# A convolution and bidirectional-scan kernel: order of the first loads, taps scaled in one operation, and additions moved to VectorE in the lone fronts

## The chip, the cores and the metric

The kernel runs on one core of a Trainium2 chip. The metric is the device time of one launch in microseconds (us); lower is better. The engines are named as in the profile: PE is TensorE (matmuls), PEld its weight loads, DVE is VectorE, ACT is ScalarE, POOL is GpSimd, SP is SyncE, which computes nothing here and issues every DMA. A queue named with a trailing q (SPq, POOLq) is an engine's sequencer.

## The reference, cut to what matters

The input is a batch of 8 images of 64 channels and 128 x 128 pixels, fp32. Two layers follow each other. Layer 0 is a filter whose nine weights per pixel come from the image itself:

```python
h = conv(x, w1, b1, pad=1); h = where(h >= 0, h, 0.2 * h)
w_lp = softmax(conv(h, w2, b2), axis=1)          # 9 weights per pixel
w_hp = delta - w_lp                               # delta: 1 at the center tap
high = sum over 9 taps of shifted(x) * w_hp[tap]
x = x + high
```

Layer 1 normalizes over the channels, runs two bidirectional Mamba blocks over the 16384 pixels as a sequence, and ends with a residual convolution, a depthwise gate and a feed-forward part (FFN):

```python
x_norm = ln4d(input); seq = layernorm(tokens(x_norm))
for i in range(2): seq = bimamba_block(seq, ...)  # projections, conv1d of 4 taps, selective scan both ways
x = input + dw2(dw1(x_norm)) * (resconv(rmsnorm(seq)) + res)
x = x + ffn_out(gelu(g1) * g2)                    # g1, g2 = halves of depthwise3x3(ffn_in(ln4d(x)))
```

## The kernel before, in words

The whole program is one function, `tile_conv_seq_kernel`. It has three parts, one after the other.

**Constants.** Identity matrices, selection matrices and small vectors are made on VectorE and GpSimd. Each image buffer in DRAM has a border of zeros; `clear(x_img)` (L98, the DMA at L89) writes the zeros of the input's buffer with one DMA of 4257.5 KB, and it is the second DMA that SP issues. Then 24 small bias and norm vectors are loaded (L165 to L168).

**Weight preparation** (L188 to L358). The weights come in their natural layout and must be transposed, paired and scaled. Helpers do this: `twice` writes a weight twice side by side (one half by VectorE, L198, one by ScalarE, L199); `turned` (L204) is a matmul against the identity, or against a diagonal, which transposes and scales at once; `diagonal` (L215) builds on VectorE an identity scaled by a column of taps. For the nine FFN taps and the four taps of the scan's short convolution each tap takes one `diagonal`, one `turned` and one copy out of PSUM. The prepared weights of the front, of the mixing stage and of the FFN are stored to DRAM (`w_dram`, L289) for later loading; those of the scan stay on the chip. The scan's weights are prepared in two layers with two directions each, so in four units, with a head for each layer. In this part the order of the instructions is left to the scheduler. Its tiles lie in pools that are closed at the end of the part, and whose memory is used again.

**The stages.** Everything after that is planned in a dictionary: `at(time, phase, fn)` puts a step under a time and a phase, and the steps are issued in sorted order within `tc.manual_schedule()`, which keeps exactly this order on each engine. Scan chunks begin at time 0 and take the rest of the span. Around them lie four kinds of work: `Front` (layer 0 and the first normalization, L480 to L677), the scan (`Chunk`), `Mix` and `Ffn`. An image has NCH = 16 front chunks, planned FRONT_STEP = 24 apart. The front of image 0 begins at time -199, so its first eight chunks run before any scan chunk; these have `alone` set and hold two of their PSUM tiles in the pool `pw`, of which the scan has no use yet.

A front chunk works on 4 + 4 rows of the image. Its steps, in the names of the profile: `copy_x` (L681; 16 DMAs for an image, which copy the input into the bordered buffer), loads of two shifted windows (xa, L414), `hp` (L422 and L427, the first convolution, six groups of matmuls), `ha`/`hv` on ScalarE, `lp` (L510, L511, the logits), a softmax on VectorE, ScalarE and GpSimd (L517 to L538), `tp` (L543, transposes), `wt` on ScalarE (L547). Then for each of nine taps: `weight` spreads the tap's weights over the channels by a matmul (`wb`, L557), `weighted` multiplies them with the shifted window xb on VectorE (`t`, L561), and `gather` adds the product into PSUM by a matmul with the identity (`acc`, L566). `filtered` copies the sum out on ScalarE (`x1`, L570). Then follow the normalizations: center (`cp`, L577), means (`ms`, L452), root (`r`, on GpSimd, L461), spread (`rb`, L467) and scaling (`hc`, L585), with the pointwise convolution `dwp` (L594) between. Steps of neighbouring chunks interleave: the taps of one chunk stand beside the `hp` and `lp` of the next and the later norms of the one before.

The zeros of the border of another image buffer (`dw`, 15 DMAs at L89) are planned among the loads of the first chunks; each has 292.5 KB, the last 162.5 KB.

SP issues DMAs in program order. Each DMA signals one of eight semaphores in turn, and a DMA waits for the one that used its semaphore before, so at most eight are under way. A DMA whose destination reuses a tile waits on SP for the last user of this tile, and all DMAs behind it on SP wait too.

Of the kernel before, what the change touches and what calls it, by code (L numbers as in the profile page):

```python
# [8 lines left out]
F32 = mybir.dt.float32  # L9
# [6 lines left out]
P = 128  # L16
C = 64
# [38 lines left out]
def kernel(ctx: ExitStack, tc: tile.TileContext, a: dict, out: bass.AP):  # L56
# [38 lines left out]
    dw_img = [image(f"dw{i}") for i in range(2)]  # L95
    zero = const([C, PW], "zero")
    nc.vector.memset(zero, 0.0)
    clear(x_img)  # L98
# [89 lines left out]
    with tc.tile_pool(name="wspill", bufs=1) as fp, tc.tile_pool(name="wprep", bufs=2) as pp, \  # L188
            tc.tile_pool(name="wps", bufs=4, space=PSUM) as pps:
        wt = [fp.tile([P, n], F32, tag=f"w{i}", name=f"w{i}") for i, n in enumerate((FRONT_W, MIX_W, FFN_W))]  # L190
        w1_pair, w1_last, dw1 = front_weights(wt[0])
        (dw2_pair, dw2_last), (wres_pair, wres_last) = mix_weights(wt[1])
        wpair, wlast, wout_a, wout_b, win_b, wtap_b = ffn_weights(wt[2])

        def twice(src, n, m, k=1):

            t = pp.tile([n, k, 2, m], F32, tag=f"twice{k * m}", name="twice")
            nc.vector.tensor_copy(t[:, :, 0, :], src.rearrange("n (m k) -> n k m", k=k))  # L198
            nc.scalar.copy(t[:, :, 1, :], src.rearrange("n (m k) -> n k m", k=k))  # L199
            return t.rearrange("n k h m -> n k (h m)")  # L200

        def turned(lhsT, rhs, m, n):
            t = pps.tile([P, N], F32, tag="wps", name="turned")
            nc.tensor.matmul(t[0:m, 0:n], lhsT, rhs, start=True, stop=True)  # L204
            return t

        def to_blocks(dst, t, k, n):

            half = dst.shape[1] // 2
            nc.vector.tensor_copy(dst[0:k, 0:n], t[0:k, 0:n])  # L210
            nc.scalar.copy(dst[k : 2 * k, half : half + n], t[k : 2 * k, 0:n])

        def diagonal(col, n):
            d = pp.tile([P, P], F32, tag="diag", name="diag")
            nc.vector.tensor_scalar(d[0:n, 0:n], ident[0:n, 0:n], col, None, ALU.mult)  # L215
            return d[0:n, 0:n]

        both = pp.tile([P, C], F32, tag="both", name="both", bufs=1)
        nc.vector.tensor_tensor(both, ident[:, 0:C], ident[:, C:P], ALU.add)
        for t in wt:  # L220
            nc.gpsimd.memset(t, 0.0)
        nc.gpsimd.memset(w2a, 0.0)
        nc.gpsimd.memset(w2v[0:64, :], 0.0)

        w1n = pp.tile([32, C * 9], F32, tag="w1n", name="w1n")
        nc.sync.dma_start(w1n, a["L0_conv_w1"].rearrange("o c i j -> o (c i j)"))
        w1t = twice(w1n, 32, C, 9)
        resn = pp.tile([C, C * 9], F32, tag="resn", name="resn")
        nc.sync.dma_start(resn, a["L1_conv_resconv_w"].rearrange("o c i j -> o (c i j)"))
        resv = twice(resn, C, C, 9)  # L230
        dw2n = pp.tile([P, 9], F32, tag="dw2n", name="dw2n")
        for h in range(2):
            nc.sync.dma_start(
                dw2n[h * C : (h + 1) * C, :], a["L1_conv_dw2_w"].rearrange("c o i j -> c (o i j)")
            )
        for k in range(9):
            i, j = divmod(k, 3)
            t1 = turned(w1t[:, k, :], ident[0:32, 0:32], P, 32)
            tr = turned(resv[:, k, :], ident[0:C, 0:C], P, C)
            if j < 2:  # L240
                lo = slice(C * j, C * j + C)
                nc.vector.tensor_copy(w1_pair[lo, i, :], t1[lo, 0:32])
                nc.scalar.copy(wres_pair[lo, i, :], tr[lo, 0:C])
                nc.vector.tensor_scalar(dw2_pair[lo, i, :], ident[lo, lo], dw2n[lo, k : k + 1], None, ALU.mult)
            else:
                nc.vector.tensor_copy(w1_last[:, i, :], t1[:, 0:32])
                nc.scalar.copy(wres_last[:, i, :], tr[:, 0:C])
                nc.vector.tensor_scalar(dw2_last[:, i, :], both, dw2n[:, k : k + 1], None, ALU.mult)
        w2n = pp.tile([9, 32], F32, tag="w2n", name="w2n")
        nc.sync.dma_start(w2n, a["L0_conv_w2"].rearrange("o c i j -> o (c i j)"))  # L250
        to_blocks(w2a, turned(twice(w2n, 9, 32)[:, 0, :], ident[0:9, 0:9], 64, 9), 32, 9)
        nc.vector.tensor_scalar(w2v[0:64, :], w2a, 0.6, None, ALU.mult)
        nc.vector.tensor_scalar(w2a, w2a, 0.4, None, ALU.mult)
        dw1n = pp.tile([C, C], F32, tag="dw1n", name="dw1n")
        nc.sync.dma_start(dw1n, a["L1_conv_dw1_w"].rearrange("o c i j -> o (c i j)"))
        to_blocks(dw1, turned(twice(dw1n, C, C)[:, 0, :], ident[0:C, 0:C], P, C), C, C)

        fw = a["L1_conv_ffn_in_w"].rearrange("o c i j -> o (c i j)")  # L260
        fd = a["L1_conv_ffn_dw_w"].rearrange("o c i j -> o (c i j)")
        outn = pp.tile([C, HID], F32, tag="outn", name="outn")
        nc.sync.dma_start(outn, a["L1_conv_ffn_out_w"].rearrange("o c i j -> o (c i j)"))
        nc.scalar.copy(wout_a, turned(outn[:, 0:P], ident[0:C, 0:C], P, C)[:, 0:C])
        t = turned(outn[:, P:HID], ident[0:C, 0:C], REST_HID, C)
        for h in range(2):
            nc.scalar.copy(wout_b[C * h : C * h + REST_HID, :], t[0:REST_HID, 0:C])
        for g, c0, r0, n in ((0, 0, 0, P), (1, 0, HID, P), (2, 0, HID + P, REST_HID), (2, C, P, REST_HID)):
            fn = pp.tile([P, C], F32, tag="fn", name="fn")
            nc.sync.dma_start(fn[0:n, :], fw[r0 : r0 + n, :])  # L270
            fdn = pp.tile([P, 9], F32, tag="fdn", name="fdn")
            nc.sync.dma_start(fdn[0:n, :], fd[r0 : r0 + n, :])
            if g == 2:

                nc.scalar.copy(win_b[:, c0 : c0 + n], turned(fn[0:n, :], ident[0:n, 0:n], C, n)[0:C, 0:n])
                for h in range(2):
                    k0 = 9 * (c0 > 0)
                    nc.sync.dma_start(wtap_b[C * h : C * h + n, k0 : k0 + 9], fd[r0 : r0 + n, :])
            fn2 = twice(fn[0:n, :], n, C)[:, 0, :]
            for k in range(9):  # L280
                i, j = divmod(k, 3)
                t = turned(fn2, diagonal(fdn[0:n, k : k + 1], n), P, n)
                if j < 2:
                    lo = C * j
                    nc.vector.tensor_copy(wpair[lo : lo + C, i, g, c0 : c0 + n], t[lo : lo + C, 0:n])
                else:
                    nc.vector.tensor_copy(wlast[:, i, g, c0 : c0 + n], t[:, 0:n])
        for src, dst in zip(wt, w_dram):
            nc.sync.dma_start(dst, src)  # L289


        sel_d = fp.tile([P, G, P], F32, tag="sel_d", name="sel_d")
        negmask = fp.tile([P, G], F32, tag="negmask", name="negmask")
        nc.vector.tensor_reduce(
            negmask.rearrange("p (n o) -> p n o", o=1), ident.rearrange("p (d n) -> p n d", n=G), AX.X, ALU.add
        )
        nc.vector.tensor_scalar(negmask, negmask, -1.0, None, ALU.mult)
        for g in range(G):
            nc.vector.tensor_copy(
                sel_d[:, g, :].rearrange("k (d n) -> k d n", n=G),  # L300
                ident[:, 32 * g : 32 * g + 32].rearrange("k (d o) -> k d o", o=1).to_broadcast([P, 32, G]),
            )

        for l in range(DEPTH):
            nw = pp.tile([P, 1], F32, tag="nw", name="nw")
            for h in range(2):
                nc.sync.dma_start(nw[h * C : (h + 1) * C, :], row(a["L1_conv_m_norm_w"][l]))
            inx = pp.tile([DI, C], F32, tag="inx", name="inx")
            nc.sync.dma_start(inx, a["L1_conv_in_proj_w"][l, 0:DI, :])
            inz = pp.tile([DI, C], F32, tag="inz", name="inz")  # L310
            nc.sync.dma_start(inz, a["L1_conv_in_proj_w"][l, DI : 2 * DI, :])
            inx2 = twice(inx, DI, C)[:, 0, :]
            t = turned(twice(inz, DI, C)[:, 0, :], ident, P, DI)
            nc.vector.tensor_scalar(wz[:, l, :], t[:, 0:DI], nw, None, ALU.mult)
            on = pp.tile([C, DI], F32, tag="on", name="on")
            nc.sync.dma_start(on, a["L1_conv_outproj_w"][l])
            for g in range(2):
                to_blocks(
                    wo[:, l, g].rearrange("p i c -> p (i c)"),
# [160 lines left out]
    class Front:  # L480
# [82 lines left out]
        def gather(self, k):  # L563
            if k == 0:
                self.acc = acc_tile("acc")
# [772 lines left out]
```

## Time and profile before

| what | value |
|---|---|
| time, median of 3 runs | 29515.6 us (29510.37 to 29532.13) |
| the profiled execution's own time | 29464.12 us |
| its span | 29462.3 us |
| mean clock granted to PE | 0.866 of full |
| busy: POOL, DVE, PE, ACT | 94%, 93%, 80%, 63% |
| first weight load issued (w1n, L226) | 39.96 us |
| first instruction of weight preparation, last one | 41.79 us, 123.3 us |
| copies of image 0 issued | 111.09 to 140.8 us |
| first hp, first tap product | 155.52 us, 184.69 us |
| x1 copied out (L570), lone chunks | 201.31, 247.58, 292.23, 336.80, 381.28, 428.39, 472.98, 524.76 us |
| first operation of the scan on POOL, on DVE | 529.84 us, 539.04 us |

The profiled execution is one run; its time stands 51 us below the median of the three timed runs. A table of stretches gives for each the busy time of every engine with the number of its instructions, the clock, and the share of time in which the DMA engines were busy. A timeline row gives the start, the duration, the engine, the line, and what is written from what; in square brackets stands how long the engine was idle before it, and what ended this. A row of the waits gives the waiting instruction, what it waited for, the sum in us, the number of times and the longest.

### The profile page before, as it was taken

How to read it: one execution, taken by the hardware profiler on the slowest of the kernel's cores; microseconds unless marked ns; L12 is line 12 of the kernel's file. 1: busy time of each engine (PE TensorE's matmuls, PEld its weight loads, DVE VectorE, ACT ScalarE, POOL GpSimd, SP SyncE). 2: the span in 40 equal slices, each digit the busy share in tenths (PEclk: the TensorE clock that was granted, in tenths of full speed). 3: DMA queues.
4: the chain of work that ended last, by engine and by line, in shares of the span. 5: the costliest groups of instructions: out<-in, count | busy, mean ns of one | idle time of the engine just before them, and what ended most of it. 6: DMA issues, size and time to landing. Idle time of an engine off the chain costs nothing. (4 is left out here: it accounts for less than half of the span.)

```text
span 29462.3 us, 312607 instructions
## 1 busy us (share of the span) xinstructions
PE 23428.5 (80%) x97852; PEld 7363.8 (25%) x97852; DVE 27280.7 (93%) x17559; ACT 18566.1 (63%) x28357; POOL 27653.4 (94%) x8732
## 2 busy tenths in 40 slices
PE   7666888878788787887878878787787878878678
PEld 3211222223222232222322223222222222222123
DVE  4999999999999999999999999999999999999997
ACT  3666666666666666666666666666666666666663
POOL 3999999999999999999999999999999999999993
PEclk8777888988889888988889888898888988889789
DMA  4676677767777677776787767777677776777674
GB/s 114 221 245 219 226 246 242 240 217 230 249 241 237 216 234 254 239 233 217 235 256 235 233 219 237 251 239 229 221 239 247 236 228 219 246 246 238 217 250 142
DMA packets 2592281, 6762.83 MB, mean 230 GB/s; under 512 B 431270, under 2 KB 736822, under 8 KB 2589462
## 3 DMA queue, kind: packets, MB, share of 16 engines
q1 hardware_dynamic: 2590614, 6742.83, 70.7%
q8 instruction: 774, 12.68, 0.2%
q14 instruction: 893, 7.32, 0.1%
HBM read 5509.49 MB, written 1265.19 MB: 230 GB/s over the span
## 5 line engine op out<-in xcount | busy, mean ns | idle before, releaser
L1089 POOL TENSOR_TENSOR bu<-dup,bp 128x2048 f32<-128x2048 f32 x4096 | 18584.8, 4543 | 373.6 <-DVE w L1117 231.0
L1097 ACT ACTIVATE w<-dtp,a_neg 128x1024 f32<-128x1024 f32 x8192 | 9159.6, 1118 | 793.8 <-DVE hs L1115 334.7
L1136 POOL TENSOR_TENSOR hs<-hs,cp 128x1024 f32<-128x1024 f32 x2832 | 6693.9, 2364 | 236.0 <-ACT state L1129 183.1
L1139 DVE TENSOR_TENSOR hs<-w,cp 128x1024 f32<-128x1024 f32 x5360 | 6562.4, 1224 | 317.2 <-DMA cp<-bc_dram 88.5
L1117 DVE TENSOR_TENSOR_SCAN w<-w,state,bu 128x1024 f32<-128x1024 f32 x2683 | 6290.5, 2345 | 302.1 <-ACT w L1097 301.0
L1115 DVE TENSOR_TENSOR_SCAN w<-w,state,bu 128x1024 f32<-128x1024 f32 x2677 | 6278.7, 2345 | 250.2 <-ACT w L1097 248.8
L1155 PE MATMUL y<-hs,sel_y 128*32 128x512 f32 x32768 | 5126.6, 701 | 55.3 <-POOL hs L1136 55.1
L1129 ACT COPY state<-w 128x1 f32<-128x1 f32 x5360 | 838.0, 156 | 5484.9 <-DVE hs L1139 5433.5
L1117 DVE TENSOR_TENSOR_SCAN hs<-w,state,bu 128x1024 f32<-128x1024 f32 x1413 | 3308.4, 2341 | 183.3 <-issue 121.2
L1115 DVE TENSOR_TENSOR_SCAN hs<-w,state,bu 128x1024 f32<-128x1024 f32 x1419 | 3321.2, 2340 | 38.6 <-PE y L1155 17.5
L1148 PE MATMUL y<-xc,dskip 128*64 128x512 f32 x4096 | 1571.0, 856 | 1656.3 <-ACT yv L1172 1383.9
L967 PE MATMUL xp<-hn,wx 128*128 128x512 f32 x4096 | 2353.8, 704 | 653.6 <-ACT xc L973 476.2
L799 PE MATMUL fp<-fw,bgw 128*128 128x512 f32 (+1 forms) x5760 | 2272.1, 636 | 105.9 <-ACT ga L846 66.2
L1129 ACT COPY state<-hs 128x1 f32<-128x1 f32 x2832 | 541.2, 191 | 1937.8 <-DVE hs L1117 989.9
L1155 PEld LDWEIGHTS y<-hs,sel_y 128*32 128x32 f32 x32768 | 730.1, 117 | 3666.8 <-issue 2458.0
L1008 PE MATMUL dp<-xc,wdt 128*128 128x512 f32 x2048 | 1226.9, 683 | 463.8 <-ACT dt L1015 373.0
L461 POOL TENSOR_TENSOR r<-r,neg_half 128x8 f32<-128x8 f32 x768 | 1265.8, 1649 | 318.2 <-ACT r L458 299.2
L1097 ACT ACT_TABLE_LOAD x1134 | 1454.9, 1283 | 20.5
L566 PE MATMUL acc<-t,ident 128*128 128x512 f32 x2304 | 1370.9, 680 | 99.3 <-DVE hc L585 94.7
L805 PE MATMUL fp<-fw,bgw 64*128 64x512 f32 (+1 forms) x5760 | 1415.1, 609 | 0.0
L1045 POOL TENSOR_TENSOR dt<-dt,xc 128x1024 f32<-128x1024 f32 x512 | 1214.9, 2373 | 173.2 <-DMA dt_dram<-dt 154.7
L967 PEld LDWEIGHTS xp<-hn,wx 128*128 128x128 f32 x4096 | 830.6, 216 | 1967.7 <-issue 961.4
(211 smaller groups left out, 25729.1 us busy)
## 6 DMA issues: line engine op xcount, KB each, us to landing
bp<-bc_dram SPq DMA_DIRECT2D x4096, 256.0 KB
dup<-du_dram SPq DMA_DIRECT2D x4096, 256.0 KB
dtp<-dt_dram SPq DMA_DIRECT2D x4096, 256.0 KB
cp<-bc_dram SPq DMA_DIRECT2D x4096, 256.0 KB
hn<-hn_dram SPq DMA_DIRECT2D x1024, 256.5 KB
dt_dram<-dt SPq DMA_DIRECT2D x512, 512.0 KB
du_dram<-dt SPq DMA_DIRECT2D x512, 512.0 KB
yf_dram<-yv SPq DMA_DIRECT2D x512, 256.0 KB
```

Of the source, the lines that this page charges most:

```text
L799: nc.tensor.matmul(o, wpair[:, i, g, m], self.win[h][:, i : i + ROWS, 0:W], start=(i == 0), stop=False)
L805: nc.tensor.matmul(o, wlast[rows, i, g, m], self.win[h][rows, i : i + ROWS, lo : W + lo], start=False, stop=(i == 2),)
L967: nc.tensor.matmul(self.xp[h], wx[:, self.l, self.d, i, :], self.hn2[:, s.start + 2 * i : s.stop + 2 * i], start=(i == 0), stop=(i == 1),)
L1089: nc.gpsimd.tensor_tensor(bu, self.dup[self.pairs[k][1]], self.over_pair("bp", k), ALU.mult)
L1097: nc.scalar.activation(w, self.dtp[gp][:, i, :], AF.Exp, scale=a_neg[:, self.l, self.d, g, j : j + 1])
L1115: nc.vector.tensor_tensor_scan(to, w, bu, s0, ALU.mult, ALU.add)
L1117: nc.vector.tensor_tensor_scan(to[:, ::-1], w[:, ::-1], bu[:, ::-1], s0, ALU.mult, ALU.add)
L1129: nc.scalar.copy(self.column(u), h[:, T - 1 : T] if self.d == 0 else h[:, 0:1])
L1136: nc.gpsimd.tensor_tensor(hs, hs, c, ALU.mult)
L1139: nc.vector.tensor_tensor(hs, w, c, ALU.mult)
L1148: nc.tensor.matmul(self.y[C * h : C * h + C, :], dskip[:, self.l, self.d, C * gp : C * gp + C], self.xc[:, s], start=True, stop=False,)
L1155: nc.tensor.matmul(self.y[lo : lo + 32, :], sel_y, hs[:, i, s], start=False, stop=(k % 4 == 3))
```

## The change

It has three parts.

1. *Order of the loads.* `clear(x_img)` is taken from the constants. The weight preparation is put within `tc.manual_schedule()`, so its instructions keep the order in which they are written. At its beginning stand all loads of the front, mixing and FFN weights; behind them on SP the clear and the 16 copies of image 0; then the rest: the tap loads of the FFN (`wtap_b`), the stores of the prepared weights, the loads of the scan's weights. `plan_front` copies the image only for the later images. The tiles `fn` and `fdn` have four buffers instead of two.
2. *Taps.* `diagonal` is gone. `by_taps` multiplies a block of rows with all its taps in one VectorE operation (128 x 1152 for the FFN, 128 x 512 for the scan's convolution), and `turned` then transposes each tap's part against the identity. The copies of the third column of FFN taps (`wlast`) go from VectorE to ScalarE.
3. *Additions.* In a lone front chunk `gather` no longer uses TensorE: the first product's tile becomes `x1`, and each further product is added to it on VectorE. There is no copy out of PSUM for these chunks. In the other chunks nothing changes.

```diff
@@ constants
+    def copy_x(b, i):
+        r = W // NCH
+        nc.sync.dma_start(pixels(x_img)[:, 1 + r * i : 1 + r * i + r, 1 : W + 1], x[b, :, r * i : r * i + r, :])
     nc.vector.memset(zero, 0.0)
-    clear(x_img)
@@ weight preparation, now within tc.manual_schedule()
-        def diagonal(col, n):
-            d = pp.tile([P, P], F32, tag="diag", name="diag")
-            nc.vector.tensor_scalar(d[0:n, 0:n], ident[0:n, 0:n], col, None, ALU.mult)
-            return d[0:n, 0:n]
+            def by_taps(rows, taps, n, k):
+                m = rows.shape[1]
+                t = pp.tile([P, k, m], F32, tag=f"taps{k}", name="taps")
+                nc.vector.tensor_tensor(
+                    t[0:n], rows.rearrange("n (o m) -> n o m", o=1).to_broadcast([n, k, m]),
+                    taps.rearrange("n (k o) -> n k o", o=1).to_broadcast([n, k, m]), ALU.mult,
+                )
+                return t[0:n]
...
+            for part in ((0, 0, 0, P), (1, 0, HID, P), (2, 0, HID + P, REST_HID), (2, C, P, REST_HID)):
+                _, _, r0, n = part
+                fn = pp.tile([P, C], F32, tag="fn", name="fn", bufs=4)
+                nc.sync.dma_start(fn[0:n, :], fw[r0 : r0 + n, :])
+                fdn = pp.tile([P, 9], F32, tag="fdn", name="fdn", bufs=4)
+                nc.sync.dma_start(fdn[0:n, :], fd[r0 : r0 + n, :])
+                parts.append((part, fn, fdn))
+            clear(x_img)
+            for i in range(NCH):
+                copy_x(0, i)
...
-            fn2 = twice(fn[0:n, :], n, C)[:, 0, :]
+                fn2 = by_taps(twice(fn[0:n, :], n, C)[:, 0, :], fdn[0:n, :], n, 9)
-                t = turned(fn2, diagonal(fdn[0:n, k : k + 1], n), P, n)
+                    t = turned(fn2[:, k, :], ident[0:n, 0:n], P, n)
-                    nc.vector.tensor_copy(wlast[:, i, g, c0 : c0 + n], t[:, 0:n])
+                        nc.scalar.copy(wlast[:, i, g, c0 : c0 + n], t[:, 0:n])
...
-                    t = turned(inx2, diagonal(cw[:, j : j + 1], DI), P, DI)
+                    taps = by_taps(inx2, cw, DI, KC)
+                        t = turned(taps[:, j, :], ident, P, DI)
@@ class Front
         def gather(self, k):
+            if self.alone and k == 0:
+                self.x1 = self.t.pop(k)
+            elif self.alone:
+                nc.vector.tensor_tensor(self.x1, self.x1, self.t.pop(k), ALU.add)
+            if self.alone:
+                return
             if k == 0:
                 self.acc = acc_tile("acc")
             nc.tensor.matmul(self.acc, ident, self.t.pop(k), start=(k == 0), stop=(k == 8))
         def filtered(self):
-            self.x1 = tmp("x1")
-            nc.scalar.copy(self.x1, self.acc)
+            if not self.alone:
+                self.x1 = tmp("x1")
+                nc.scalar.copy(self.x1, self.acc)
@@ plan_front
-        for i in range(NCH):
+        for i in range(NCH if b else 0):
             at(a - FRONT_STEP - 24 + i, REST, copy_x, b, i)
```

## The prediction

> **What bounds the kernel now.** I read first the table of busy time by stretches of the span (length, busy time of PE, PE loads, DVE, ACT and POOL, then clock, DMA share, GB/s).
>
> ```profile
> 0.00:42.00 42.00, 0.00 (x0) 0.00 (x0) 8.24 (x32) 1.49 (x2) 4.43 (x12) 1.00 0.72 108
> 42.00:124.00 82.00, 61.42 (x220) 49.30 (x220) 38.44 (x184) 12.98 (x52) 0.00 (x0) 1.00 0.28 47
> 202.00:474.00 272.00, 226.70 (x890) 109.94 (x892) 52.65 (x95) 52.86 (x115) 34.94 (x36) 0.75 0.18 49
> 540.00:1000.00 460.00, 348.00 (x1482) 114.43 (x1480) 429.55 (x293) 292.41 (x466) 449.57 (x154) 0.83 0.68 220
> ```
>
> From 540 us on GpSimd and VectorE are full (449.6 and 429.6 of 460 us), and the change touches nothing there. All it can win lies in the 539 us before the first scan (539.04): 42 us of waiting for weights, 82 us of weight preparation, a load stage, and from 185 to 525 us eight lone fronts, where PE is busiest and VectorE fills 19%. The stages follow one another, so a microsecond saved here shifts all that follows.
>
> Second, the timeline of SP's queue (start, duration; consecutive alike rows merged).
>
> ```profile
> 1.99 22.86 SPq L165 DMA_DIRECT2D v_norm_w<-in_L_conv_norm_w  x1
> 39.96 0.31 SPq L226 DMA_DIRECT2D w1n<-in_L_conv_w  x1
> 111.09 29.73 SPq L681 DMA_DIRECT2D x_dram<-in_x  x16
> 140.93 4.89 SPq L414 DMA_DIRECT2D xa<-x_dram  x4
> 147.73 0.33 SPq L477 DMA_DIRECT2D bgw<-w_dram  x1
> 174.18 3.01 SPq L435 DMA_DIRECT2D xb<-x_dram  x2
> ```
>
> The load after the image clear is stuck for 22.86 us, so w1n goes out at 39.96. The image copies go out last, behind all weights, and hold the first xa load to 140.93.
>
> Third, the timelines of VectorE and TensorE about the first and second lone chunk.
>
> ```profile
> 41.79 0.70 DVE L198 COPY twice<-w1n 32x576 f32<-32x576 f32 x1 [32.26 <-DMA w1n<-in_L_conv_w]
> 184.69 0.69 DVE L561 TENSOR_TENSOR t<-xb,wb 128x512 f32<-128x512 f32 x1 [15.81 <-DMA xa<-x_dram]
> ...
> 201.95 2.07 PE L577 MATMUL cp<-x,center 128*128 128x512 f32 x2 [0.68 <-ACT x L570]
> 249.19 2.07 PE L577 MATMUL cp<-x,center 128*128 128x512 f32 x2
> ```
>
> The first tap product waits for a DMA until 184.69 (xb is what it reads). The adding matmuls run to 201.5; one lone chunk follows another after about 45 us (the copies at L570 lie 46.3, 44.7, 44.6, 44.5, 47.1, 44.6 and 51.8 apart). Fourth, the waits and groups up to 600 us:
>
> ```profile
> DVE t L561 <- PE wb L557: 139.1, 57, 12.7
> ACT x L570 <- PE acc L566: 101.1, 7, 19.6
> L566 PE MATMUL acc<-t,ident 128*128 128x512 f32 x162 | 106.0, 751 | 8.7 <-DVE hc L585 4.4 <-DVE t L561 4.3
> L561 DVE TENSOR_TENSOR t<-xb,wb 128x512 f32<-128x512 f32 x81 | 54.8, 685 | 154.9 <-PE wb L557 139.1 <-DMA xa<-x_dram 15.8
> ```
>
> Products wait for weights (wb), which stand on PE behind adding matmuls of two passes, 751 ns each. That loop is what the third part opens.
>
> [...] after 32.5 us of idleness the first two hp groups take 2.01 and 1.78 us, the others 1.05. [...] Here w1n lands 1.83 us after issue. [...] the trace's 22.86 us is used.
>
> **Part 1, the order of loads.** Removed: the clear ahead of the weights. The 24 small loads take some 0.62 us each, so w1n goes out at about 15.8 and lands at 17.6, 24 us earlier. Front and mix weights took 12.9 us (41.8 to 54.7). Moved: clear and 16 copies now stand behind the early weights but ahead of everything else on SP: the tap loads (wtap), the three weight stores, the scan's (mamba) weights, then xa. The clear goes out near 22.3 and runs 28 us, to 50; the first copy waits for that. Copies took 37.4 us of data (111.1 to 148.5), so they end at 88; wtap lands near 89.5, its store (3.5 us before) follows, inx lands at about 95. FFN preparation should be over by 63, so PE then idles 32 us for inx, which before was loaded at 58.3, ahead of its use.
>
> What decides is the wait in front of the first xa load. In both kernels its buffer lies where weight preparation had its tiles, so it waits for the last VectorE instruction of the preparation. Before, this cost nothing: preparation ended at 123.3, the copies were issued till 140.8. Now it comes last, and behind it on SP stand bgw, 15 clears of dw (4.2 MB), xa and xb of the first chunks; PE's first hp waits on them. Preparation of the mamba weights took 35.7 us (87.6 to 123.3), 7.1 us for each of four units and some 4 us for each of two heads. In written order a unit's tap operation stands behind VectorE's tail of the unit before (reduce, dskip, 0.69 us for the taps, about 1.4 us with hand-overs), and PE waits: 4 x 8.4 + 2 x 4.1 = 41.8 us. End: 95 + 42 = 137 (bounds 129 and 147).
>
> From the first data of xa (148.5, when the copies were through) to xb's landing (184.5) were 36 us for 6.25 MB: DMA-bound. From 137, with 1.5 us of start: xb at 174.5. **Gain 10 us** (0 to 18). So most of the 25 us won at the start is spent waiting for inx and for the preparation.
>
> **Part 2, taps in one operation.** 36 diagonals of 254 ns go; 4 operations of 1.36 us come, and 36 pairs that took about 1 us a tap fall to PE's 0.575 us: some 10 us less FFN preparation, 12 copies moved to ACT at no cost (ACT is busy 13 of 82 us). But FFN ends at 63, and inx comes at 95: worth nothing by itself. The cover is those 32 us; without it 10 us would show. For the mamba's taps it is in the 8.4 above.
>
> **Part 3, adding on VectorE.** Per lone chunk: nine matmuls of 2 passes and an ACT copy of 0.58 us go, eight VectorE additions of 0.685 us come (5.5 us; the trace has independent ones 0.61 to 0.65 apart; one that directly follows the addition it depends on, two per chunk, it doesn't show: between that and 0.9). They stand ahead of the next mx and hc scaling on VectorE. The odd wb still waits for the product before it, since two share one PSUM buffer.
> First chunk: 17.26 us from t0 to cp (184.69 to 201.95) become 17 operations x 0.63 + 1 = 11.7: 5.5 us. Second period: 47.2 becomes 42.5: 4.7.
> Then five periods, counted from the tp transposes (at 266.82 in the second). t0 at +3.6, hc at +7.3, t1 and t2 to +9, two additions to +10.4; wb3 stands behind the ms means at +11.3, then t3 at +12, and one product or addition each 0.63 us: a8 ends at +19.6. lp starts at +17.1 behind wb8, takes 2.6 us warm (4.9 cold), rb 1.8 to 2.0: cp at +21.5 to +24, against +27.3. From cp to tp were 17.6 us after a warm PE, 20.0 in the colder first round; I take 18.6. So 22.4 + 18.6 = 41.0 against 45.0: 4 us (1.5 to 5.5), five times: **20 us**. The last stretch, where the scan's projections share PE: 0.5 us lost matmul time, no more: 0.5 later to 1.7 earlier; I take 0.3 later.
>
> **The sum**: 10 + 5.5 + 4.7 + 20 - 0.3 = 40 us. Against the profiled execution (29464.12 us for a span of 29462.3) that gives 29424. The median shown is 51 us above that execution (its own spread is 22), and I subtract from it: 29515.6 - 40 = **29475.6**.
>
> **Rivals.**
> A, the forecast, with 30 to 52 us gained: 29464 to 29486.
> B, the start gives nothing: preparation ends at 147 or later (a unit over 10.5 us), xb at 184. Additions alone: 30 us, 29486 (to 29500 if periods give 1.5). For it: strict order, cold PE, and loads queued behind 4 MB of copies. Against it: 7.1 us a unit before.
> C, both work better: the mamba preparation needs no more than its 35.7 us and PE stays warm: 16 + 6 + 6 + 26 + 2 = 56 us, 29460; with xa freed earlier than I read, up to 70, 29446. For it: PE's own work in a unit is only some 6.3 us. Against it: the wb spacing leaves PE idle between weights.
> D, the clock turns it: without the adding matmuls PE never warms in a lone chunk. Then per chunk hp costs 5.6 us more (six groups at 1.92 instead of 0.98), lp 2.3, ms, rb and the rest 1.8: 9.7 against about 5 won. Seven chunks lose 33 us, the start wins 10: 23 us slower, 29539. It decides from the point where hp's own six groups don't warm PE; at 155.5 two were enough after 32 us of idleness, which speaks against it.
> That the change doesn't act as said isn't a case: the instructions are in the kernel.
>
> **Chances.** A 0.55, B 0.20, C 0.20, D 0.05. 0.2% is 59 us, about what a measurement of this kernel can tell from no change. Faster by more is the upper part of C and a tail of A: 0.17. Slower by more needs D with the start lost too: 0.02. Within: 0.81. The range takes in A, most of B and C with their bounds: 29446 to 29502.
>
> **What would show it.** w1n at 16 and twice at 18; copies issued from 50, ended by 88; a stretch of PE idleness up to about 95; the first xa near 137, directly behind the preparation's last VectorE instruction; t0 at 174.5; cp of the first chunk 12 us later; chunk distances of 41 us; first scan at 499. Wrong if xa is issued near 90 or t0 stays at 184, if the chunks lie 45 us apart with hp groups at 1.9, or if the steady rate after the first scan differs.

## The result, and the profile after

| | before | after |
|---|---|---|
| median of 12 runs each | 29514.4 us (29497.7 to 29532.1) | 29480.6 us (29454.5 to 29498.0) |
| ratio to before, 95% interval | | 0.9988 (0.9980 to 0.9995) |
| profiled execution, its span | 29464.1, 29462.3 us | 29481.4, 29479.5 us |
| first product (t) | 184.69 us | 189.57 us |
| first cp, second, seventh | 201.95, 249.19, 474.71 us | 202.33, 245.69, 451.30 us |
| first scan on VectorE | 539.04 us | 514.23 us |

The kernel became 34 us faster (15 to 59 by the interval); 40 were forecast. In the profiled pair the scan starts 24.8 us sooner, and yet the profiled span after is 17 us *longer*: from the first scan to the end the kernels took 28923 and 28965 us. In the fourteen profiles of this study that last part lies between 28907 and 28965 us, for the changed kernel alone at 28965, 28907 and 28935. It scatters by more than the change is worth, and it goes with the occasion, not with the kernel (see "The same chip" below); its cause is not shown. The profile of before is evidently not of the same occasion as its times: 29464.1 us lies below all twelve of them. So the experiments below are read at two marks ahead of that last part, the first product and the first scan, and the medians are only their check.

The table of stretches after (columns as before):

```profile
0.00:42.00 42.00, 17.40 (x68) 14.98 (x69) 18.11 (x62) 8.11 (x24) 4.43 (x12) 1.00 0.56 75
42.00:124.00 82.00, 21.28 (x96) 17.85 (x95) 15.02 (x54) 5.34 (x26) 0.00 (x0) 0.53 0.89 98
202.00:474.00 272.00, 198.98 (x854) 102.99 (x854) 83.16 (x149) 57.00 (x124) 37.43 (x40) 0.67 0.21 55
540.00:1000.00 460.00, 353.88 (x1499) 119.08 (x1500) 438.20 (x301) 291.38 (x461) 452.89 (x154) 0.84 0.69 220
```

The first 42 us now hold weight preparation; in the next 82 PE, which had been busy for 61 us, works 21: it waits. In the lone fronts VectorE's busy time rises from 53 to 83 us of 272. After 540 us GpSimd and VectorE are as full as before (453 and 438 us of 460, against 450 and 430).

SP's queue after:

```profile
15.17 0.31 SPq L228 DMA_DIRECT2D w1n<-in_L_conv_w  x1
22.88 0.59 SPq L89 DMA_DIRECT2D x_dram<-zero  x1
23.51 24.18 SPq L387 DMA_DIRECT2D hn_dram<-zero  x1
55.38 32.80 SPq L98 DMA_DIRECT2D x_dram<-in_x  x16
103.52 0.73 SPq L325 DMA_DIRECT2D inx<-in_L_conv_in_proj_w  x1
147.03 2.38 SPq L431 DMA_DIRECT2D xa<-x_dram  x4
176.06 3.14 SPq L452 DMA_DIRECT2D xb<-x_dram  x2
```

and VectorE at the scan's weights, at the end of the preparation and at the first product:

```profile
106.45 0.20 DVE L202 COPY twice<-inx 128x64 f32<-128x64 f32 x1 [50.28 <-DMA inx<-in_L_conv_in_proj_w]
146.61 0.28 DVE L375 TENSOR_SCALAR dskip<-ident,dp 128x128 f32<-128x128 f32 x1
189.57 0.69 DVE L578 TENSOR_TENSOR t<-xb,wb 128x512 f32<-128x512 f32 x1 [22.20 <-DMA xa<-x_dram]
```

w1n goes out 25 us sooner, and FFN preparation is over at 55 us. Then VectorE waits 50.28 us for inx, which stands behind the image copies. The preparation ends with the dskip at 146.61 + 0.28, and at 147.03 SP issues the first xa, after a wait of 18.2 us for just this dskip. This is the wait on reused memory. The first line below is from SP's own waits up to 200 us; the others show where time is saved in the lone fronts, by waits and groups up to 600 us:

```profile
SPq L431 <- DVE dskip L375: 18.2, 1, 18.2
DVE t L578 <- PE wb L574: 83.0, 16, 12.7
L578 DVE TENSOR_TENSOR t<-xb,wb 128x512 f32<-128x512 f32 x81 | 54.0, 682 | 107.7 <-PE wb L574 83.0 <-DMA xa<-x_dram 23.6
L584 DVE TENSOR_TENSOR t<-t 128x512 f32<-128x512 f32 x64 | 45.9, 717 | 0.6
```

Products wait 83 us for weights instead of 139, and additions start with no wait behind them (0.6 us in all).

### The profile page after: what moved, and what is told of

Read it like the earlier page. It is cut to its first block, busy times and chain, and to the rows that moved or that the text cites. A ratio compares the mean times of both kernels' runs of the same rounds, so it can differ in the third digit from the quotient of the medians.

```text
span 29479.5 us, 312296 instructions
## 1 busy us (share of the span) xinstructions
PE 23358.6 (79%) x97708; PEld 7341.1 (25%) x97708; DVE 27316.3 (93%) x17567; ACT 18561.4 (63%) x28361; POOL 27648.1 (94%) x8732
## 5 line engine op out<-in xcount | busy, mean ns | idle before, releaser
L589 PE MATMUL acc<-t,ident 128*128 128x512 f32 x2160 | 1265.5, 669 | 85.6 <-DVE hc L609 84.7
```

## The experiments

My theory after the result: the additions win about 30 us, the start as a whole gives or takes a few, since the new order makes the scan's weights late and the first xa waits for the end of their preparation. The rivals: the order of loads gains and the additions cancel out; or the transfers set the start whatever the order. All kernels of one group below ran on the same chip.

### The additions, alone and left out

`adds_only` is the kernel before with only the new `gather` and `filtered`; `no_adds` is the changed kernel with the old ones.

> Only the additions on VectorE, on the kernel before. If the parts add up as the two traces read: the first tap product stays at 184.7 us, first chunk to cp 12.8 us instead of 17.3, chunk distances 41 to 43 us, first scan at about 509 us instead of 539.0; median 30 us below before (under the kernel with all three parts, which starts its scan at 514.2). Rival, the load order brings the gain and the additions cancel out (colder TensorE): first scan at 536 to 542, median as before.

> All but the additions: load order and taps in one operation, sums by matmul. If the new order loses time at the start: first tap product at 189.6 us, first scan at about 544, median 5 us above before, not to be told from it. Rival, the order gains and something in the lone chunks hides it: first scan at 529 or sooner.

| | first product | first scan | distance | median, ratio (interval) |
|---|---|---|---|---|
| adds_only | 198.39 | 523.55 | 325.2 | 29485.4, 0.9994 (0.9985 to 1.0002) |
| no_adds | 191.71 | 546.12 | 354.4 | 29505.3, 0.9997 (0.9989 to 1.0005) |

The distance from first product to first scan is 354.4 us in both kernels with adding matmuls (before: 354.35), 324.7 and 325.2 in both with additions: 29 to 30 us, in whichever kernel. The rival of cancelling additions falls, by the marks; the medians alone don't decide, since both intervals include no change.

But I missed one thing: the start of adds_only, whose instructions up to the first product are those of before, came 13.7 us later than in the profile of before, and so its scan came at 523.55 instead of the expected 509. Starts of different occasions can't be compared. Those of these two runs can, since they ran on one chip: adds_only has the start of before, no_adds that of the changed kernel, which comes 6.7 us sooner (191.71 against 198.39). So the theory that the new start loses time is wrong here, although no_adds met its expected times within 3 us.

### The same chip, twice the same kernels

So both kernels were profiled again together, unchanged, with two more of the next question.

> The kernel before, profiled on the same chip as the next three, since its start came out 14 us later in the run with the additions alone (first tap product 198.4 us) than in its own profile (184.7). If the start varies from run to run: first tap product anywhere from 184 to 199; the distance from there to the first scan 354 us within 1. Rival, the additions changed the start: 184 to 186 again.

> The changed kernel on the same chip. If the start is DMA-bound and varies: first tap product between 187 and 193, distance to the first scan 324.5 within 1. If the new order truly costs 5 us at the start: it lies 3 to 7 us after that of the kernel before on this chip; if it gains: sooner than that.

Before:

```profile
186.92 0.69 DVE L561 TENSOR_TENSOR t<-xb,wb 128x512 f32<-128x512 f32 x1 [16.51 <-DMA xa<-x_dram]
```

with the first scan at 543.37. After:

```profile
139.59 0.28 DVE L375 TENSOR_SCALAR dskip<-ident,dp 128x128 f32<-128x128 f32 x1
177.34 0.69 DVE L578 TENSOR_TENSOR t<-xb,wb 128x512 f32<-128x512 f32 x1 [16.73 <-DMA dw_dram<-zero]
```

with the first scan at 502.34. On this chip the start gains 9.6 us and the scan starts 41.0 sooner. The distances between the marks are 356.5 and 325.0 us, so the additions win 31.4; I had expected 354 within 1 for the kernel before, and a first product of 187 to 193 for the changed one. The image copies were issued in 29.3 us, not 32.8, and the scan's weights arrived at 99.4, not 106.5: the same instructions move 12 us by the pace of the transfers. A third profile of the changed kernel on another occasion had 177.93 and 504.62, a distance of 326.7, which is 2 us more than expected.

The 4.9 us that the first pair of profiles shows as lost are of this kind. Its image copies were issued in 29.73 us before and in 32.80 after. On the chip of adds_only and no_adds this took 32.7 to 33.5 us, on this one 29.0 to 29.5. So the first pair sets a start with fast transfers against one with slow ones. The part after the first scan goes the same way: 28948 to 28965 us in the four profiles of adds_only's chip and the first one of the changed kernel, 28907 to 28935 in the nine others. That slow transfers lengthen it is not shown.

> The changed kernel once more, as the measure for the next three on this chip: first tap product between 177 and 190 us, 324.5 us from there to the first scan.

### The taps, alone and left out; the order, left out

`taps_only` is the kernel before with `by_taps` and the copies on ScalarE; `diag` is the changed kernel with `diagonal` put back; `taps_adds` is the kernel before with the second and third part, so the changed kernel without its order:

```diff
-            fn2 = twice(fn[0:n, :], n, C)[:, 0, :]
+            fn2 = by_taps(twice(fn[0:n, :], n, C)[:, 0, :], fdn[0:n, :], n, 9)
-                t = turned(fn2, diagonal(fdn[0:n, k : k + 1], n), P, n)
+                t = turned(fn2[:, k, :], ident[0:n, 0:n], P, n)
```

> Only the taps in one operation, on the kernel before (scheduler's order, image copies last). Theory (the operation shortens the FFN preparation, and before nothing stood in front to hide it): preparation and image copies some 8 to 12 us sooner than in the kernel before on this chip, first tap product and first scan the same 8 to 12 us sooner. Rival (the copies out of PSUM and TensorE's cold passes set the pace, not the diagonals): within 3 us.

> The changed kernel with a diagonal and a matmul for every tap again (in written order, image copies ahead of the scan's weights, additions on VectorE). Theory (TensorE waits for the scan's weights anyway): FFN preparation 8 to 15 us later than in the changed kernel but before the scan's weights land, end of preparation within 4 us of the changed kernel's 147, first tap product within 4 us. Rival (strict order makes each tap wait): end of preparation 10 us later or more.

> Taps in one operation and additions on VectorE, on the kernel before: the changed kernel without its new order (scheduler's order in the preparation, image copies last). Theory (the new order costs: taps alone began their products 21 us sooner than the kernel before, the whole change only 9.6 sooner on that chip): first tap product 8 to 15 us sooner than in the changed kernel on this chip, first scan the same, median some 10 us below the changed kernel's and 50 below before. Rival (the new order is what gains at the start): first tap product later than in the changed kernel.

| | end of preparation | first xa issued | first product | first scan |
|---|---|---|---|---|
| before_again | 124.3 | 141.63 | 186.92 | 543.37 |
| taps_only | 104.0 | 120.70 | 165.92 | 522.26 |
| diag | 152.6 | 152.70 | 191.24 | 517.20 |
| after_again | 139.9 | 140.01 | 177.34 | 502.34 |
| after_third | 139.6 | 139.72 | 177.93 | 504.62 |
| taps_adds | 104.9 | 121.25 | 166.70 | 491.87 |

(The last two are of another group than the first four.) taps_only, VectorE and SP:

```profile
103.81 0.16 DVE L357 TENSOR_REDUCE a_neg<-am 128x4 f32<-128x16 f32 x1
165.92 0.69 DVE L567 TENSOR_TENSOR t<-xb,wb 128x512 f32<-128x512 f32 x1 [16.26 <-DMA xb<-x_dram]
91.65 28.95 SPq L687 DMA_DIRECT2D x_dram<-in_x  x16
```

The taps alone win 21.0 us at the first product, twice what I had expected. About 1 us of this isn't theirs, since in this run the first weights were used at 41.87 us instead of 42.87. FFN preparation got some 17 us shorter (its last copy on VectorE at 70.6 instead of 88.5, with the earlier start in it), that of the scan's weights 2.5, and the image copies, which stood behind the weight loads on SP, left at 91.65 instead of 112. PE at the first FFN taps, before_again and taps_only:

```profile
58.96 1.19 PE L204 MATMUL turned<-diag,twice 128*128 128x128 f32 x4 [0.78 <-DVE diag L215]
60.81 1.19 PE L204 MATMUL turned<-diag,twice 128*128 128x128 f32 x4 [0.66 <-DVE diag L215]
56.44 8.23 PE L204 MATMUL turned<-ident,taps 128*128 128x128 f32 x36
```

Two taps took 1.85 us, of which 0.66 to 0.78 were a wait for the diagonals; now 18 take 8.23 us without a wait, 0.46 each. In the changed kernel the taps are worth 13.9 us, by another way than I thought. diag's FFN preparation ended at 81.5, still ahead of inx (100.4), so that part is covered, as forecast; but in written order each of the scan's taps waits too. PE in diag, with what ended the idle time before each:

```profile
115.89 0.77 PE L208 MATMUL turned<-diag,twice 128*128 128x128 f32 x2 [0.95 <-DVE diag L219]
117.50 0.77 PE L208 MATMUL turned<-diag,twice 128*128 128x128 f32 x2 [0.84 <-DVE diag L219]
118.98 0.77 PE L208 MATMUL turned<-diag,twice 128*128 128x128 f32 x2 [0.72 <-DVE diag L219]
120.61 0.77 PE L208 MATMUL turned<-diag,twice 128*128 128x128 f32 x2 [0.86 <-DVE diag L219]
```

against the four taps in one run of after_again:

```profile
104.57 2.04 PE L208 MATMUL turned<-ident,taps 128*128 128x128 f32 x8 [1.00 <-DVE taps L221]
```

From the head of one layer to that of the next lie 26.0 us in diag, 20.2 in after_again. My expectation of 4 us was wrong there, the rival (10 us or more) right. And diag against before_again is the order alone, since their starts have the same taps: it loses 4.3 us (191.24 against 186.92).

taps_adds settles the order beside the new taps:

```profile
166.70 0.69 DVE L567 TENSOR_TENSOR t<-xb,wb 128x512 f32<-128x512 f32 x1 [16.50 <-DMA xa<-x_dram]
```

Without the order the first product comes 11.2 us sooner than in the changed kernel on the same chip (166.70 against 177.93), the first scan 12.8. Its median is 29422.7 us against 29470.7 of before, 0.9984 (0.9977 to 0.9990). So the gain of 9.6 us at the start is +21 from the taps and -11 from the order, or, with the order first, -4 and +14.

"Order" here is two things that no run takes apart: the late loads, and the written order within the preparation. Under the written order the scan's weights took 40.4 us, in taps_only, where the scheduler orders them, 33.4; so up to 7 of the 11 us may be due to it.

### Why the order loses: the wait at xa, and what stands in front of it

`xa_apart` opens the pool of the image windows ahead of the preparation's pools, so that its memory is not reused. `mamba_first` puts the loads of the scan's weights behind the clear and ahead of the copies (with buffers for all four units).

```diff
+    inp = ctx.enter_context(tc.tile_pool(name="in", bufs=2))
     with tc.tile_pool(name="wspill", bufs=1) as fp, tc.tile_pool(name="wprep", bufs=2) as pp, \
```

> The pool of the image windows is opened ahead of the weight preparation, so xa has memory of its own; nothing else changes. Theory (the wait in front of xa costs, for the reused memory): first xa at about 129 us, right behind the scan's weight loads, first tap product at about 171 to 173 instead of 189.6, first scan at about 497; median 17 us below the changed kernel. Rival (the first hp stands on TensorE behind the whole preparation anyway, so xa's wait is covered): first tap product at 185 to 190.

> The scan's weight loads ahead of the image copies, behind the clear; the rest as in the changed kernel. Theory (the scan's weights behind 4 MB of copies make the preparation late, and the first xa load waits for its end): preparation ends at about 98 us instead of 146.9, copies are over at about 110, first xa at about 115 instead of 147, first tap product at about 157 instead of 189.6, first scan at about 482; median 32 us below the changed kernel. Rival, the transfers decide and not the preparation: copies 20 us later push everything, first tap product at 185 or later, first scan at 510 or later.

On this chip the start of the changed order stood at 191.71 (no_adds). xa_apart, SP, PE and VectorE:

```profile
130.54 2.51 SPq L431 DMA_DIRECT2D xa<-x_dram  x4
148.19 1.92 PE L439 MATMUL hp<-xa,bgw 128*32 128x512 f32 x4
148.59 0.28 DVE L376 TENSOR_SCALAR dskip<-ident,dp 128x128 f32<-128x128 f32 x1
172.07 0.69 DVE L578 TENSOR_TENSOR t<-xb,wb 128x512 f32<-128x512 f32 x1 [10.56 <-DMA xb<-x_dram]
```

xa is issued 18.8 us sooner than in no_adds; hp starts on PE without any wait, right behind the preparation's last matmul, and the product comes 19.6 us sooner, at 172.07 as expected. The first scan is at 496.23, the median 0.9985 (0.9977 to 0.9992) of before. The wait was real, and the transfers now run beside the preparation.

```profile
97.82 0.28 DVE L383 TENSOR_SCALAR dskip<-ident,dp 128x128 f32<-128x128 f32 x1
72.82 33.45 SPq L98 DMA_DIRECT2D x_dram<-in_x  x16
124.98 2.39 SPq L439 DMA_DIRECT2D xa<-x_dram  x4
166.74 0.69 DVE L586 TENSOR_TENSOR t<-xb,wb 128x512 f32<-128x512 f32 x1 [21.68 <-DMA xa<-x_dram]
```

In mamba_first preparation ends at 98 us, and the first product comes 25 us sooner; the first scan is at 491.32, the median 0.9981 (0.9973 to 0.9988). xa is no longer held by the preparation (27 us pass between), but by what stands behind the copies from 106.4 us on: tap loads, the stores of the prepared weights and the zeros of hn. So it goes out 10 us later than the 115 that I had expected, and the product, expected at 157, is 10 us late too.

The changed kernel itself was not run on this chip. By their medians, 0.9985 and 0.9981 of before, these two can't be told from it (0.9988 in its own group); the marks tell them apart.

### The zeros in front of the first windows, and an order by need

`dw_late` spreads the clears of dw; `best2` joins it with mamba_first, loads the tap weights with the front's (for which the tiles are zeroed at the very start), and stores the prepared weights ahead of the copies.

```diff
-    for t, step, img in ((FIRST_FRONT_AT - 20, 2, dw_img[0]), ...
+    for t, step, img in ((FIRST_FRONT_AT + 8, FRONT_STEP, dw_img[0]), ...
```

> The changed kernel with the clears of the dw image spread over the chunks, each ahead of its chunk's store, instead of in front of the second xa and the first xb. Theory (from the first xa to the first product the transfers set the pace, 4.2 of 6.3 MB are these zeros): from the first xa's issue to the first product 24 to 28 us instead of 37 to 42, first scan 11 to 16 us sooner than in the changed kernel on this chip. Rival (TensorE's chain hp, lp, hp, tp sets it): less than 4 us.

> The changed kernel with the loads in an order by need: front, FFN and tap weights, clear, the scan's weights, stores of the prepared weights, image copies, xa directly behind them; clears of the dw image spread as in the run before. Theory: preparation ends near 98, copies are issued from about 73 to 103 and xa at about 107, first product at 134 to 142 instead of 177 to 190, first scan at 459 to 467; median 75 us below before, which is 0.25% and beyond what the measurement leaves open. Rival (something else comes late behind the loads, the clear or the stores): first product at 155 or later.

The first product in dw_late:

```profile
170.13 0.69 DVE L578 TENSOR_TENSOR t<-xb,wb 128x512 f32<-128x512 f32 x1 [9.57 <-PE wb L574]
```

From the first xa's issue to the first product 29.9 us pass instead of 38.2, where 24 to 28 were expected. The product comes at 170.13, 7.8 us sooner than in after_third, the scan at 495.35, 9.3 sooner; ratio 0.9980 (0.9974 to 0.9987). At the scan this is less than the 11 to 16 expected and more than the rival's 4: with the zeros gone, the product no longer waits for a DMA but for wb, so PE's chain takes over after 8 us. And best2:

```profile
99.08 0.28 DVE L384 TENSOR_SCALAR dskip<-ident,dp 128x128 f32<-128x128 f32 x1
72.75 31.74 SPq L98 DMA_DIRECT2D x_dram<-in_x  x16
114.40 2.80 SPq L440 DMA_DIRECT2D xa<-x_dram  x4
145.01 0.69 DVE L587 TENSOR_TENSOR t<-xb,wb 128x512 f32<-128x512 f32 x1 [9.48 <-PE wb L583]
470.38 2.35 DVE L1144 TENSOR_TENSOR_SCAN hs<-w,state,bu 128x1024 f32<-128x1024 f32 x1 [1.11 <-ACT w L1126]
```

The first scan is at 470.4, 34.2 us sooner than in the changed kernel on the same chip; xa was issued 7 us later than I had put it, since six small DMAs for hn stand behind the copies (104.5 to 112.8), and the last two of them and xa wait for copies still under way, 4.9 us in all. So the first product and the first scan lie 3 us outside their expected ranges (134 to 142 and 459 to 467). The median is 29391.5 us against 29470.7 of before, ratio 0.9976 (0.9966 to 0.9987): 79 us by the medians, the lowest ratio of the study. That it lies under taps_adds and dw_late by their medians is within the intervals; by the first scan it is 21 and 25 us ahead of them.

## Why the prediction was right, point by point

**Where the gain can lie.** Right: the change shows in nothing after the first scan. (The adding matmuls of the first chunk end at 201.27, not at 201.5; nothing rests on it.)

**Part 1.** w1n was forecast at 15.8 and came at 15.17. Preparation of the FFN ended at 55, not 63; copies began at 55.4 (53.1 on the second chip), not 50; inx was used at 106.5 (99.4), not 95. The preparation of the scan's weights took 40.4 us (forecast 41.8), so it ended at 146.9 (139.9) instead of 137. That the first xa waits for it is shown twice: by SP's wait of 18.2 us and by xa_apart. From the preparation's end to the first product 42.7 us (37.5), forecast 37.5. Gain: 9.6 us on one chip, 6.7 on another; forecast 10, bounds 0 to 18. The first pair of profiles, -4.9, meets a sign that I had named for being wrong ("t0 stays at 184"), but it compares unlike transfers. That 9.6 came so close is partly luck: the end of the preparation was 2.9 us later than forecast, and so was the start of before on that chip, by 2.2.

**Part 2.** Here a step failed: "worth nothing by itself". It cost FFN diagonals at 10 us beside a cover of 32 us and saw nothing more. Alone, the taps win 21.0 us; in the new order 13.9. Two terms were mis-sized. The FFN part is some 17 us, not 10: my 10 come out as 36 x 0.425 less 5.4 us for the four new operations (they took 1.35 to 1.36 us each in taps_only), but these run beside PE's passes, which wait for none of them there, and a tap takes 0.40 us on PE (36 from 56.44 to 70.96), not 0.575 (in the profile before two took 1.05 to 1.22). And the scan's taps I had put into 8.4 us a unit without asking what they would cost as diagonals in written order. The sum at the start was right because those 8.4 us already had the taps as one operation in them. The 10 us are 21 won by the taps less 11 lost by the order; I had written them down as the order's, which alone loses 4.3.

**Part 3.** Right in place and size:

| | before | after | gain | forecast |
|---|---|---|---|---|
| first product to first cp | 17.26 | 12.76 | 4.5 | 5.5 |
| to the second cp | 47.24 | 43.36 | 3.9 | 4.7 |
| five periods | 225.52 | 205.61 | 19.9 | 20 |
| seventh cp to first scan | 64.33 | 62.93 | 1.4 | -0.3 |
| sum | | | 29.7 | 29.9 |

The 29.7 us are differences within each kernel's own profile, so the unlike starts don't enter. A period is 41.1 us, forecast 41.0, with errors that offset: tp to cp is 23.5 (22.4 forecast), cp to tp 17.7 on average (18.6). Rival D's colder TensorE shows in lp, as it had put it, but not in hp: over the lp ahead of the second cp the granted clock was 0.50 after (238.80 to 243.05 us) and 1.00 before (243.92 to 246.42), over the hp behind it 1.00 in both (249.44 to 255.40 after, 252.93 to 258.90 before). PE before (first line) and after, about the second cp:

```profile
244.80 0.39 PE L511 MATMUL lp<-w2a,ha 64*128 64x18 f32 x2
...
239.18 0.61 PE L528 MATMUL lp<-w2a,ha 64*128 64x18 f32 x2
...
243.79 1.98 PE L484 MATMUL rb<-ident,r 128*64 128x128 f32 x16 [0.75 <-DVE lg L536]
245.69 2.08 PE L601 MATMUL cp<-t,center 128*128 128x512 f32 x2
...
249.44 1.05 PE L439 MATMUL hp<-xa,bgw 128*32 128x512 f32 x4
250.42 1.05 PE L444 MATMUL hp<-xa,bgw 64*32 64x512 f32 x4
```

A pair of lp matmuls takes 0.61 us instead of 0.39, so lp takes 4.2 us instead of 2.6; and rb, whose PSUM tile was lp's, waits 0.75 us until VectorE has read the logits. I had lp between 2.6 and 4.9 and no wait at rb. From the second cp on all hp groups of the lone fronts run at 1.05, as before. (Behind the first cp, from 206.88 us after and 206.51 before, two of six take 1.92 in both kernels, at a granted clock of 0.76.) In the five periods behind the second cp the clock was the same again: after, 0.50 over lp and 1.00 over hp; before, 1.00 over both. Why it fell and what brought it back is not shown.

**The rivals.** The measured 34 us with its interval of 15 to 59 admits both A (40 us) and B (start gives nothing, 30 us). The two comparisons on one chip speak for A: the start gives 9.6 and 6.7 us, the additions 29 to 31. C needed a preparation of 35.7 us; it took 40.4. D is out: from the second cp on hp takes 1.05 us a group, at a granted clock of 1.00.

## What to carry to other kernels

Moving a load forward also moves back what stands behind it in the same queue (inx here, issued at 103.52 us instead of 58.34): list the queue anew, with the waits in front of each DMA, and look for the one that is last next. A buffer that reuses the memory of a closed pool carries the end of that pool's work into the queue; opening the pool earlier (18.8 us here) or ordering the loads by need (25 us) removes a wait that a faster preparation only shortens. And where the total scatters by more than the change, compare a mark ahead of the scatter, on one chip.

## What the runs showed that I had not expected

- The same instructions at the start took 177.3 to 189.6 us to the first product in three profiles of the changed kernel, and 184.7 to 198.4 in three profiles with the start of before; the distance from there to the first scan agreed within 3 us for the same kernel. Starts that transfers set are to be compared on one chip only.
- A DMA issued behind the clear of 4257.5 KB held SP for 22.9 to 24.2 us, wherever the clear stood (two behind it together 24.5 in best2 and 25.4 in mamba_first). In the changed kernel this is a small DMA for hn, and the copies wait for the clear anyway (5.7 us in the first profile).
- An addition that directly follows the one it depends on cost little more than an independent operation: two such took 1.41 us together (192.14 us in the first profile after), two products 1.28 (193.47).
